# Cross-attention with layernorm: score matmuls on 32x128 tiles of the array, epsilon on GpSimd, and a new order within a pair

## The chip, the cores and the metric

The kernel runs on one core of a Trainium2 chip. A core has five engines with an instruction stream each: TensorE (PE; its weight loads are shown as PEld), VectorE (DVE), ScalarE (ACT), GpSimd (POOL) and SyncE (SP, which here only issues transfers). They work side by side and wait for one another through semaphores. The metric is the device time of one execution in microseconds (us). The kernel before takes 521.16 us (median of three: 519.04, 521.16, 522.03).

## The reference, cut to what matters

`x` is 8192 rows of 512 in float32 (four batches of 2048), `ctx` has 77 rows of 512 per batch and is key and value at once; the mask hides some of the 77 keys. There are 16 heads of 32.

```python
qs  = (x   @ wq).reshape(B, Lq, 16, 32).transpose(0, 2, 1, 3)
ks_ = (ctx @ wk).reshape(B, 77, 16, 32).transpose(0, 2, 1, 3)
vs  = (ctx @ wv).reshape(B, 77, 16, 32).transpose(0, 2, 1, 3)
scores = einsum('bhqd,bhkd->bhqk', qs, ks_) / sqrt(32)
scores = where(mask[:, None], -inf, scores)
attn   = einsum('bhqk,bhkd->bhqd', softmax(scores), vs)
out    = attn.transpose(0, 2, 1, 3).reshape(B, Lq, 512) @ wo + x
mu, var = mean(out), mean((out - mean(out)) ** 2)
y = (out - mu) / sqrt(var + 1e-5) * gamma + beta
```

## The kernel before, in words

The 8192 rows are 64 tiles of 128 rows, and the tiles go in pairs: pair n is tiles 2n and 2n + 1. Tiles 0 to 5 are done by a loop of their own at the start, together with the loads of the weights and the keys and values of the four batches. Pairs 3 to 26 (24 of them) all run through one list of words, the string `PAIR` (L47 to L51). Tiles 54 to 63 follow a longer written list, `ORDER`. Each word names a function, a tile, visit or pair relative to the current one, and at times a part. The order in which the words are issued is the order of each engine's instruction stream; there is no further scheduler, and buffers are given out in the same order.

What a pair does, with the letters of the words:

- `Q`, `q`: a *visit* computes q for 128 rows' worth of columns on TensorE (L186, 12 matmuls; float32 is made of high and low parts, hence three products of each) and VectorE copies it out of PSUM (L203). `g`, `i`, `j` load xT and split it into the two parts (load on SP, high part on ScalarE L175, low part on GpSimd L179).
- `S`, `D`: the scores of the pair, as q times keys, head by head (L310). The contraction is over the 32 columns of a head, so a matmul uses 32 rows of the array, and heads j = 0 to 3 of a group lie in four row groups of it. In the kernel before each score of 128 rows is two matmuls, for rows 0 to 63 and 64 to 127, each on a 32x64 tile of the array. Each float32 matmul shows as two records (two weight loads and two matmuls). A pair has 32 scores (16 heads, two tiles): `S` does 24 of them and `D` the other 8. They lie in six PSUM banks: four of their own, `sc` 0 to 3, and two shared ones, `sc_e` and `sc_f`.
- `T`: the maximum of a head's masked scores, on VectorE (L353; `T1.30` is for the two heads of the second tile that lie in `sc_f`); it writes masked scores to `pbuf` and the maxima `nm`. `e`: exponentials and their sums on ScalarE (L368). `r`: the sums' reciprocals on VectorE (L374). `n`: the multiplication by them on GpSimd (L379).
- `t`: a transpose on VectorE (L402) into `B`; `P`: its regrouping by 12 transfers on SP's queue (L414) into `PT`. `V`: attention times values, on TensorE (L448). `a`, `b`: its result is split into a high part AH on ScalarE (L497) and a low part AL on VectorE (L501).
- `O`: the output projection, 12 matmuls a tile on TensorE (L546). `+`: the residual, on VectorE (L549). `s`: mean and variance (L554, L559), and for the second tile of a pair the variance plus epsilon (L561, VectorE), its power −1/2 and two products (L562 to L564, GpSimd). `k`: scaling on ScalarE (L570). `f`: gamma and beta on GpSimd (L574, L575). `w` stores the tile (L578), `x` loads the residual (L518), both on SP.
- `L`, `B`: the mask of the next batch is loaded (L288, SP) and turned into a bias of −3e38 or 0 (L294, VectorE). This happens in three pairs, n = 6, 14 and 22 for `B`.

On TensorE a pair of the string is always S, D, O-6, O-5, Q5, Q6, V-2: the pair's own scores, the output of the tiles three pairs earlier, the visits of the next pairs, and av of the pair two earlier. PSUM has eight banks, handed out in a ring.

The lines that the change touches most:

```python
def score(t, g, j, half):
    r0 = (t % 4) * P + half
    return nc.tensor.matmul(
        scs[t][g, j][half : half + P // 2],
        qd[t // 4][q, g, r0 : r0 + P // 2], ...)
```

Of the kernel before, what the change touches and what calls it, by code (L numbers as in the profile page):

```python
# [13 lines left out]
ALU = mybir.AluOpType  # L14
# [3 lines left out]
P = 128  # L18
D = 512
# [7 lines left out]
GH = 4  # L27
# [7 lines left out]
EPS = 1.0e-5  # L35
# [5 lines left out]
JOIN = 6  # L41
# [3 lines left out]


PAIR = """  # L47
q4 k-8 a-3.1 f-8 i4 x-4 S T1.30 b-3.0 L T0.1 D e0.1 b-3.1 T0.0 T1.31 T1.3 x-3 T0.3 O-6 T1.10 T0.2 e0.0 T1.11 T1.14
+-6 T1.1 e0.3 s-6 O-5 t-1 e1.15 e0.2 r0 Q5 j4 g5 Q6 n0 e1.3 e1.10 +-5 q5 B e1.14 e1.1 e1.11 k-7 V-2 s-5 w-8 t0 r1 n1
P-1 f-7 w-7 a-2.0  # L50
"""  # L51
JOINT = """ a24.1 b24.0 b24.1 """

# [23 lines left out]
def xattn_layernorm(  # L77
# [15 lines left out]
    nc = tc.nc  # L93
# [35 lines left out]
    small = const.tile([P, 128], F32, name="small")  # L129
# [1 line left out]
    warm = ident.bitcast(BF16)  # L131
    ident = ident[:, :P]
    unit = ident.bitcast(F32R)
    mhalf, mneg, gates, meps = small[:, 0:2], small[:, 2:4], small[:, 4:5], small[:, 5:6]
    last_st = small[:, 8:20].rearrange("p (n s) -> p n s", n=2)
    pbuf = [const.tile([P, NP, PW], F32, name=f"pbuf{i}") for i in range(NPB)]

# [25 lines left out]
    fx, gx, qd, qp, bat, pts = {}, {}, {}, {}, {}, {}  # L163
    scs, nmax, sums, bts, at, pas = {}, {}, {}, {}, {}, {}
# [132 lines left out]
    def scores(t):  # L297
        nmax[t] = sb.tile([P, H], F32, tag="nm", bufs=3, name=f"nm_{t}")
        sums[t] = sb.tile([P, H], F32, tag="sum", bufs=3, name=f"sum_{t}")
        sc = [bank(f"sc_{t}_{j}") for j in range(GH)]  # L300
        scs[t] = {(g, j): sc[j][:, g * NK : (g + 1) * NK] for g in range(NG) for j in range(GH)}
        for g in range(NG):
            for half in range(0, P, P // 2):
                for j in range(GH):
                    score(t, g, j, half)

    def score(t, g, j, half):
        q = slice(HD * j, HD * (j + 1))
        r0 = (t % 4) * P + half
        return nc.tensor.matmul(  # L310
            scs[t][g, j][half : half + P // 2],
            qd[t // 4][q, g, r0 : r0 + P // 2],
            kct[q, g, t // TPB, keys_of(j)],
            start=True,
            stop=True,
        )

    def scores_pair(b):
# [6 lines left out]
        units = []  # L325
# [225 lines left out]
    def moments(t):  # L551
        b, tt = divmod(t, 2)
# [5 lines left out]
        mv, rn = mvs[b], rns[b]  # L558
        nc.vector.bn_aggr(mv[:, tt, :], st)  # L559
        if tt == 1:  # L560
            nc.vector.tensor_scalar(rn[:, 0, :], mv[:, :, 1], EPS, None, ALU.add)  # L561
            nc.gpsimd.tensor_tensor(rn[:, 0, :], rn[:, 0, :], mhalf, ALU.pow)  # L562
            nc.gpsimd.tensor_tensor(rn[:, 1, :], mv[:, :, 0], rn[:, 0, :], ALU.mult)
            nc.gpsimd.tensor_tensor(rn[:, 1, :], rn[:, 1, :], mneg, ALU.mult)  # L564
# [50 lines left out]
    def rsqrt_one(t):  # L615
        mv = mvs[t, 1]
        if t in summed:
            nc.gpsimd.tensor_scalar(mv[:, 2:3], mv[:, 1:2], 1.0 / D, meps, ALU.mult, ALU.add)
        else:
            nc.gpsimd.tensor_tensor(mv[:, 2:3], mv[:, 1:2], meps, ALU.add)  # L620
        nc.gpsimd.tensor_tensor(mv[:, 2:3], mv[:, 2:3], mhalf[:, :1], ALU.pow)

    def bias_one(t):
# [361 lines left out]
```

## Time and profile before

| | |
|---|---|
| median of three | 521.16 us |
| profiled execution | 520.62 us, span 518.8 us |
| granted TensorE clock, mean | 0.995 |
| TensorE busy | 498.5 us (96%), 6864 matmul records |
| VectorE / ScalarE / GpSimd busy | 469.7 / 471.3 / 420.1 us |
| score matmuls (L310) into the four own banks | 3312 records, mean 238 ns |
| instruction queue q8 | 54 packets, 0.88 MB |
| epsilon on VectorE (L561) | 24 times, mean 309 ns |

The span is the profiled execution from its first to its last event; 1.8 us lie outside it. Busy times overlap, since the engines work side by side: an engine at 96% of the span leaves little for others to shorten, unless what it waits for is found. A row of the table of waits reads: who waited, on which line, for which engine and line, with total, number and longest. "issue" is a wait that ended with no event that the profile shows. The chain of waits follows the work that ended last back through what released it, and its pieces are shown in order of time as start, length and what it was.

### The profile page before, as it was taken

To read this page: it belongs to the slowest core of one execution; us is meant where nothing else is said; L and a number is where in the kernel's file an instruction comes from. 1 tells how busy PE (TensorE), PEld (TensorE's weight loads), DVE (VectorE), ACT (ScalarE), POOL (GpSimd) and SP (SyncE) were. 2 spreads that over 40 slices of the span, in tenths; PEclk is the share of its full clock that TensorE was granted. 3 is DMA by queue.
4 is the path that set the end of the run, shared out by engine and by line. 5 is a ranking of instruction groups with operands and counts; after the bars stand their busy time and mean duration, and the time that the engine had idled before them with its cause. 6 is when DMAs were issued, how large, how long until landed. Compare 5 with 4: busy or idle time off the path is not lost.

```text
span 518.8 us, 20291 instructions
## 1 busy us (share of the span) xinstructions
PE 498.5 (96%) x6864; PEld 391.3 (75%) x6864; DVE 469.7 (91%) x2581; ACT 471.3 (91%) x2239; POOL 420.1 (81%) x359
## 2 busy tenths in 40 slices
PE   8999899999999999999999999989998999999994
PEld 6987578776777877776788777767876777777784
DVE  6698989899989999999999999998997899999997
ACT  6798989988999999998999999998999799999861
POOL 0659356887988989887998898887989688999894
PEclk9999999999999999999999999999998999999999
DMA  8946856696887888698688868788687778767665
GB/s 303 399 146 162 217 150 183 180 249 165 224 231 199 220 205 234 181 251 229 180 230 223 225 169 241 209 236 223 192 219 190 185 214 241 178 175 209 164 204 202
DMA packets 58279, 109.48 MB, mean 211 GB/s; under 512 B 9203, under 2 KB 10739, under 8 KB 58176
## 3 DMA queue, kind: packets, MB, share of 16 engines
q1 hardware_dynamic: 55776, 103.35, 71.4%
q0 software_dynamic: 1872, 4.20, 2.8%
q8 instruction: 54, 0.88, 0.8%
q10 hardware_dynamic: 528, 0.66, 0.4%
q14 instruction: 49, 0.40, 0.2%
HBM read 41.68 MB, written 16.78 MB: 113 GB/s over the span
## 4 chain that ended last, share of the span: by engine, by line
PE 79%; DVE 8%; DMA 5%; ACT 3%; issue 2%; SPq 2%; DVEq 0%; ACTq 0%
PE pq L186 27%; PE po L546 26%; PE pa L448 8%; PE sc L310 6%; PE sc L546 3%; DVE B L402 3%; DMA PT<-B 2%; ACT pbuf L368 2%; DVE pbuf L353 2%; SPq L414 2%; PE pv L252 2%; PE sc_e L310 2%; PE pk L212 1%; DMA out<-o 1%; PE pq L695 1%
## 5 line engine op out<-in xcount | busy, mean ns | idle before, releaser
L368 ACT ACTIVATE pbuf<-pbuf,nm 128x77 f32<-128x77 f32 x1024 | 352.0, 351 | 4.7 <-DVE nm L353 4.4
L368 ACT ACTIVATION_READ_ACCUMULATOR pbuf<-pbuf,nm 128x1 f32 x1024 | 196.7, 192 | 0.0
L379 POOL TENSOR_TENSOR pbuf<-pbuf,ri 128x1232 f32<-128x1232 f32 x63 | 142.1, 2256 | 53.6 <-DVE ri L374 53.0
L353 DVE CUSTOM_DVE_ANT_0 pbuf<-sc,mb 128x77 f32<-128x77 f32 x828 | 143.5, 233 | 6.4 <-PE sc L310 6.0
L186 PE MATMUL pq<-xth,wqh 128*128 128x512 f32 (+1 forms) x256 | 98.7, 386 | 0.0
L186 PE MATMUL pq<-xtl,wqh 128*128 128x512 f32 (+1 forms) x256 | 97.9, 382 | 0.0
L186 PE MATMUL pq<-xth,wql 128*128 128x512 f32 (+1 forms) x256 | 97.9, 382 | 0.0
L402 DVE STREAM_TRANSPOSE B<-pbuf 128x1280 f32<-128x1280 f32 x63 | 94.1, 1495 | 2.5 <-DMA PT<-B 1.2
L546 PE MATMUL po<-woh,AH 128*128 128x512 f32 x224 | 91.1, 407 | 0.0
L546 PE MATMUL po<-wol,AH 128*128 128x512 f32 x224 | 88.1, 393 | 0.6 <-issue 0.6
L546 PE MATMUL po<-woh,AL 128*128 128x512 f32 x224 | 87.1, 393 | 0.0
L353 DVE DVE_READ_ACCUMULATOR2_ANT nm<- 128x1 f32 x1024 | 84.5, 82 | 0.0
L575 POOL TENSOR_TENSOR o<-o,bet 128x512 f32<-128x512 f32 x53 | 68.5, 1293 | 4.2
L574 POOL TENSOR_TENSOR o<-o,gam 128x512 f32<-128x512 f32 x53 | 68.8, 1299 | 1.0 <-ACT o L570 1.0
L179 POOL TENSOR_TENSOR xtl<-xtf,xth 128x1024 fp32r<-128x1024 f32 x28 | 67.4, 2409 | 0.0
L310 PE MATMUL sc<-kct,q 32*64 32x77 f32 x3312 | 56.6, 238 | 5.2 <-issue 2.8
L448 PE MATMUL pa<-PT,vsb 96*32 96x256 f32 x960 | 58.2, 382 | 0.7 <-DMA PT<-B 0.3
L310 PEld LDWEIGHTS sc<-kct,q 32*64 32x64 f32 x3312 | 49.5, 130 | 11.3 <-issue 6.8
L186 PEld LDWEIGHTS pq<-xth,wqh 128*128 128x128 f32 x256 | 48.1, 188 | 9.7
L186 PEld LDWEIGHTS pq<-xth,wql 128*128 128x128 f32 x256 | 48.1, 188 | 9.4
L186 PEld LDWEIGHTS pq<-xtl,wqh 128*128 128x128 f32 x256 | 48.1, 188 | 9.2
L546 PEld LDWEIGHTS po<-woh,AH 128*128 128x128 f32 x224 | 42.4, 189 | 10.8 <-DVE ri L374 0.4
(170 smaller groups left out, 832.0 us busy)
## 6 DMA issues: line engine op xcount, KB each, us to landing
PT<-B SPq DMA_DIRECT2D x355, 128.0 KB
xtf<-xT SPq DMA_DIRECT2D x28, 512.0 KB
o<-x SPq DMA_DIRECT2D x56, 256.0 KB
out<-o SPq DMA_DIRECT2D x56, 256.0 KB
PT<-B POOLq DMA_DIRECT2D x16, 128.0 KB, 4.1
o_end<-x SPq DMA_DIRECT2D x7, 256.0 KB
out<-o_end SPq DMA_DIRECT2D x7, 256.0 KB
xtf<-xT SPq DMA_DIRECT2D x4, 256.0 KB
```

The source lines that it names most:

```text
L179: nc.gpsimd.tensor_tensor(l, fx.pop((g, c)), h.bitcast(F32), ALU.subtract)
L186: nc.tensor.matmul(pq, w[:, c, m * P : (m + 1) * P], r[:, c, rs], start=(n == 0), stop=(n == 11))
L252: nc.tensor.matmul(pv, ctx_s[c][i][:, r, :], v[c], start=(n == 0), stop=(n == 11))
L310: return nc.tensor.matmul(scs[t][g, j][half : half + P // 2], qd[t // 4][q, g, r0 : r0 + P // 2], kct[q, g, t // TPB, keys_of(j)], start=True,
L353: nc.vector.tensor_tensor_reduce(pb[:, i // 2, (i % 2) * NK : (i % 2 + 1) * NK], scs[t][g, j], mb[:, t % TPB, keys_of(h)], -1.0, CEIL, ALU ...
L368: nc.scalar.activation(p, p, AF.Exp, bias=nmax[t][:, i : i + 1], scale=-1.0, accum_out=sums[t][:, i : i + 1])
L379: nc.gpsimd.tensor_tensor(pv, pv, rv.to_broadcast((P, NP, 2, NK)), ALU.mult)
L402: nc.vector.transpose(bt.rearrange("p c q r -> p q c r"), pbuf[t % NPB].rearrange("p q (c r) -> p q c r", c=5),)
L448: nc.tensor.matmul(pas[b, g // 2][HD * j : HD * (j + 1), (g % 2) * BLK : (g % 2 + 1) * BLK], vsb[:, 2 * b // TPB, HD * h : HD * (h + 1)], ...
L546: nc.tensor.matmul(pos[t][:, cols], a[:, c, rs], w[:, c, cols], start=go, stop=done)
L574: nc.gpsimd.tensor_tensor(o, o, gam, ALU.mult)
L575: nc.gpsimd.tensor_tensor(o, o, bet, ALU.add)
```

## The change

Five things are edited.

1. A score of a pair is one matmul of 128 rows on a 32x128 tile of the array instead of two of 64 rows on 32x64 tiles: 32 matmuls a pair instead of 64. The single tiles at the start and the end keep the halves. In D the scores go in the order j = 0, 2, 3, 1.
2. Epsilon is added by GpSimd, from a column of constants two wide, instead of VectorE.
3. In the first pair (n = 3) O-6 stands before D.
4. In the words, `B` moves from late in the pair to right behind S, and `L` from the front to behind V-2.
5. The remaining words of VectorE, ScalarE, GpSimd and SP are reordered: f-8 behind j4, t-1 and t0 close together at the end, r0 and +-5 earlier, another order of the exponentials. On TensorE the order of a pair is as before.

```diff
--- before.py
+++ after.py
@@ -45,9 +45,9 @@
 
 
 PAIR = """
-q4 k-8 a-3.1 f-8 i4 x-4 S T1.30 b-3.0 L T0.1 D e0.1 b-3.1 T0.0 T1.31 T1.3 x-3 T0.3 O-6 T1.10 T0.2 e0.0 T1.11 T1.14
-+-6 T1.1 e0.3 s-6 O-5 t-1 e1.15 e0.2 r0 Q5 j4 g5 Q6 n0 e1.3 e1.10 +-5 q5 B e1.14 e1.1 e1.11 k-7 V-2 s-5 w-8 t0 r1 n1
-P-1 f-7 w-7 a-2.0
+q4 k-8 a-3.1 S B T1.30 b-3.0 T0.1 i4 e0.1 D x-4 T1.10 j4 T1.31 b-3.1 O-6 T0.2 T0.0 e0.2 T0.3 +-6 T1.3 T1.11 e0.0 x-3
+g5 e0.3 T1.14 e1.14 O-5 T1.1 e1.10 Q5 +-5 r0 s-6 e1.15 f-8 n0 s-5 Q6 w-8 q5 e1.1 t-1 V-2 L e1.11 t0 P-1 e1.3 k-7 r1
+n1 f-7 w-7 a-2.0
 """
 JOINT = """ a24.1 b24.0 b24.1 """
 
@@ -131,7 +131,7 @@
     warm = ident.bitcast(BF16)
     ident = ident[:, :P]
     unit = ident.bitcast(F32R)
-    mhalf, mneg, gates, meps = small[:, 0:2], small[:, 2:4], small[:, 4:5], small[:, 5:6]
+    mhalf, mneg, gates, meps = small[:, 0:2], small[:, 2:4], small[:, 4:5], small[:, 5:7]
     last_st = small[:, 8:20].rearrange("p (n s) -> p n s", n=2)
     pbuf = [const.tile([P, NP, PW], F32, name=f"pbuf{i}") for i in range(NPB)]
 
@@ -302,14 +302,14 @@
         for g in range(NG):
             for half in range(0, P, P // 2):
                 for j in range(GH):
-                    score(t, g, j, half)
-
-    def score(t, g, j, half):
+                    score(t, g, j, half, P // 2)
+
+    def score(t, g, j, r0, n):
         q = slice(HD * j, HD * (j + 1))
-        r0 = (t % 4) * P + half
-        return nc.tensor.matmul(
-            scs[t][g, j][half : half + P // 2],
-            qd[t // 4][q, g, r0 : r0 + P // 2],
+        at = (t % 4) * P + r0
+        nc.tensor.matmul(
+            scs[t][g, j][r0 : r0 + n],
+            qd[t // 4][q, g, at : at + n],
             kct[q, g, t // TPB, keys_of(j)],
             start=True,
             stop=True,
@@ -330,18 +330,15 @@
                 scs[t][g, j] = bk[:, at * NK : (at + 1) * NK]
             units.append(mine[6:] + mine[:6] if j % 2 == 0 else mine)
         for i in range(6):
-            for half in range(0, P, P // 2):
-                for j in range(GH):
-                    score(*units[j][i], j, half)
+            for j in range(GH):
+                score(*units[j][i], j, 0, P)
         held[b] = units
 
     def scores_rest(b):
         units = held.pop(b)
         for i in (6, 7):
-            for js in ((0, 2), (3, 1)):
-                for half in range(0, P, P // 2):
-                    for j in js:
-                        score(*units[j][i], j, half)
+            for j in (0, 2, 3, 1):
+                score(*units[j][i], j, 0, P)
 
     def maxima(t, lo, hi):
         pb = pbuf[t % NPB]
@@ -558,7 +555,7 @@
         mv, rn = mvs[b], rns[b]
         nc.vector.bn_aggr(mv[:, tt, :], st)
         if tt == 1:
-            nc.vector.tensor_scalar(rn[:, 0, :], mv[:, :, 1], EPS, None, ALU.add)
+            nc.gpsimd.tensor_tensor(rn[:, 0, :], mv[:, :, 1], meps, ALU.add)
             nc.gpsimd.tensor_tensor(rn[:, 0, :], rn[:, 0, :], mhalf, ALU.pow)
             nc.gpsimd.tensor_tensor(rn[:, 1, :], mv[:, :, 0], rn[:, 0, :], ALU.mult)
             nc.gpsimd.tensor_tensor(rn[:, 1, :], rn[:, 1, :], mneg, ALU.mult)
...
@@ -906,7 +903,11 @@
 
     def pair(n):
         u = 2 * n
-        for word in PAIR.split():
+        words = PAIR.split()
+        if n == JOIN // 2:
+            words.remove("O-6")
+            words.insert(words.index("D"), "O-6")
+        for word in words:
             op, k, part, queue = read(word)
             if op == "S":
                 scores_pair(n)
```

The first place is TensorE's stream in the first pair, n = 3, around D. In the names `sc_3_0` to `sc_3_3` are the pair's own four banks, `sc_3_e` and `sc_3_f` the shared ones, `po_0` and `po_1` the outputs of tiles 0 and 1. Before, the end of D and the output's start:

```order
L310 MATMUL sc_3_0_1056<-kct_71,q_1_529 64x77
L310 MATMUL sc_3_2_1058<-kct_71,q_1_529 64x77
L310 MATMUL sc_3_0_1056<-kct_71,q_1_529 64x77
L310 MATMUL sc_3_2_1058<-kct_71,q_1_529 64x77
L310 MATMUL sc_3_f_1061<-kct_71,q_1_529 64x77
L310 MATMUL sc_3_e_1060<-kct_71,q_1_529 64x77
L310 MATMUL sc_3_f_1061<-kct_71,q_1_529 64x77
L310 MATMUL sc_3_e_1060<-kct_71,q_1_529 64x77
L546 MATMUL po_0_1150<-woh_69,AH_0_953 128x512
L546 MATMUL po_0_1150<-wol_70,AH_0_953 128x512
```

Now, the end of the first output, D and the second output:

```order
L543 MATMUL po_0_1093<-woh_69,AH_0_953 128x512
L543 MATMUL po_0_1093<-wol_70,AH_0_953 128x512
L543 MATMUL po_0_1093<-woh_69,AL_0_954 128x512
L310 MATMUL sc_3_0_1053<-kct_71,q_1_529 128x77
L310 MATMUL sc_3_2_1055<-kct_71,q_1_529 128x77
L310 MATMUL sc_3_f_1058<-kct_71,q_1_529 128x77
L310 MATMUL sc_3_e_1057<-kct_71,q_1_529 128x77
L310 MATMUL sc_3_0_1053<-kct_71,q_1_529 128x77
L310 MATMUL sc_3_2_1055<-kct_71,q_1_529 128x77
L310 MATMUL sc_3_f_1058<-kct_71,q_1_529 128x77
L310 MATMUL sc_3_e_1057<-kct_71,q_1_529 128x77
L543 MATMUL po_1_1159<-woh_69,AH_0_953 128x512
```

D is eight matmuls of 128 rows, and the twelve of the first output stand ahead of it; in all other pairs D is followed by both outputs, as before.

The second place is VectorE's stream around the bias of batch 2, which pair 14 makes (`mb_2`). Before:

```order
L549 TENSOR_TENSOR o_23_3841<-po_23_4159,o_23_3841 128x512
L203 COPY q_8_3926<-pq_8_1_4181 128x512
L294 TENSOR_SCALAR mb_2_3806<-m8_2_3804 128x1536
L554 BN_STATS st_23_4247<-o_23_3841 128x6
L559 BN_AGGR mv_11_4156<-st_23_4247 128x2
L561 TENSOR_SCALAR rn_11_4157<-mv_11_4156 128x2
L402 STREAM_TRANSPOSE B_14_4255<-pbuf1_78 128x8x5x32
L374 RECIPROCAL ri_29_4257<-sum_29_4021 128x16
L203 COPY q_8_3926<-pq_8_2_4197 128x512
L353 ISA pbuf1_78,nm_31_4289<-sc_15_f_4296,mb_1_1646 128x77
```

Now:

```order
L399 STREAM_TRANSPOSE B_12_3387<-pbuf1_78 128x8x5x32
L399 STREAM_TRANSPOSE B_13_3627<-pbuf2_79 128x8x5x32
L371 RECIPROCAL ri_27_3647<-sum_27_3422 128x16
L203 COPY q_8_3583<-pq_8_0_3584 128x512
L294 TENSOR_SCALAR mb_2_3624<-m8_2_3622 128x1536
L350 ISA pbuf2_79,nm_29_3661<-sc_14_f_3668,mb_1_1720 128x77
L350 ISA nm_29_3661 128x1
L498 TENSOR_TENSOR AL_11_3654<-pa_11_0_3604,AH_11_3653 128x512
```

The bias stood behind the second visit's copy, with the statistics, a transpose, the reciprocal and the next pair's q copy behind it; now it stands between the pair's q copy and its first maxima, and the two transposes have come together ahead of the reciprocal.

The third place is SP's queue around the load of that mask. Before:

```order
L518 DMA o_22_3742<-x 128x512
L288 DMA m8_2_3804<-mask 128x1536
L518 DMA o_23_3841<-x 128x512
L170 DMA xtf_9_0_3924<-xT 128x1024
L578 DMA out<-o_18_3203 128x512
L414 DMA PT_12_3989<-B_12_3712 32x2x512 x12
```

Now:

```order
L515 DMA o_22_3472<-x 128x512
L515 DMA o_23_3519<-x 128x512
L170 DMA xtf_9_0_3521<-xT 128x1024
L575 DMA out<-o_18_2997 128x512
L288 DMA m8_2_3622<-mask 128x1536
L411 DMA PT_12_3629<-B_12_3387 32x2x512 x12
```

The mask's load was second in its pair's transfers; now it stands behind the store of tile 18, which waits for GpSimd's gamma and beta of that tile.

More of the change, by code (lines that the diff above doesn't have):

```diff
@@ L617, in rsqrt_one @@
         if t in summed:
-            nc.gpsimd.tensor_scalar(mv[:, 2:3], mv[:, 1:2], 1.0 / D, meps, ALU.mult, ALU.add)
+            nc.gpsimd.tensor_scalar(mv[:, 2:3], mv[:, 1:2], 1.0 / D, meps[:, :1], ALU.mult, ALU.add)
         else:
-            nc.gpsimd.tensor_tensor(mv[:, 2:3], mv[:, 1:2], meps, ALU.add)
+            nc.gpsimd.tensor_tensor(mv[:, 2:3], mv[:, 1:2], meps[:, :1], ALU.add)
         nc.gpsimd.tensor_tensor(mv[:, 2:3], mv[:, 2:3], mhalf[:, :1], ALU.pow)
```

## The prediction

> **What bounds the kernel now.** I read the page's busy shares first, then the chain of waits by engine, then the table of waits, then single stretches. The rows are the page's part 1, the chain's shares by engine, and four steps of the chain itself (start, duration, what):
>
> ```profile
> PE 498.5 (96%) x6864; PEld 391.3 (75%) x6864; DVE 469.7 (91%) x2581; ACT 471.3 (91%) x2239; POOL 420.1 (81%) x359
> PE 79%; DVE 8%; DMA 5%; ACT 3%; issue 2%; SPq 2%; DVEq 0%; ACTq 0%
> ...
> 245.87 5.67 PE po L546 x24
> 251.54 5.44 PE pq L186 x24
> 256.98 1.86 PE pa L448 x32
> 260.47 5.66 PE po L546 x24
> 333.98 5.68 PE po L546 x24
> ```
>
> TensorE is the bound. From 245.87 to 333.98 six pairs pass, 14.685 us each. In every one o_proj takes 5.67, the q visits 5.44 and av 1.86; what is left, 14.685 − 12.97 = 1.71, is the pair's scores. But a steady pair has little air on the other engines either. In the view by stretches (length, then busy of PE, PEld, DVE, ACT, POOL, then granted clock), one steady pair and one later stretch:
>
> ```profile
> 260.40:275.10 14.70, 14.70 (x212) 11.54 (x208) 13.86 (x80) 14.51 (x70) 13.11 (x12) 1.00 0.84 228
> 395.00:410.00 15.00, 13.64 (x62) 10.68 (x66) 11.47 (x68) 11.66 (x65) 10.37 (x9) 0.89 0.73 196
> ```
>
> ScalarE is busy 14.51 of 14.70: however short the scores get, a steady pair gives back only about 0.2 us before ScalarE sets the pace. So the gain has to come from places where PE stands still, and there are three kinds. The change acts on 24 pairs.
>
> **1. The score tiles: +2.9.** Single instructions of the timeline (start, duration, out<-in, array tile, shape):
>
> ```profile
> 245.80 0.50 PE L546 MATMUL po<-woh,AH 128*128 128x512 f32 x1
> 246.37 0.39 PE L546 MATMUL po<-woh,AL 128*128 128x512 f32 x1
> 258.78 0.28 PE L310 MATMUL sc_e<-kct,q 32*64 32x77 f32 x1
> 258.89 0.23 PE L310 MATMUL sc_e<-kct,q 32*64 32x77 f32 x1
> 258.96 0.23 PE L310 MATMUL sc_e<-kct,q 32*64 32x77 f32 x1
> 503.85 0.27 PE L529 MATMUL pa<-ident,xtl 128*128 128x128 f32 x1
> 503.96 0.27 PE L529 MATMUL pa<-ident,xth 128*128 128x128 f32 x1
> ```
>
> The first matmul after another shape shows its weight load: 0.50 − 0.39 = 0.11 us for 128 columns, 0.28 − 0.23 = 0.05 for 64. L529, whose matmuls are short, starts one every 0.11: it is bound by loads of 128 columns. Now eight score records start per 0.07 us (258.89 to 258.96), two 64-column halves of each of four row groups side by side, so that rhythm is the stream of 77 columns. A pair has 128 records (64 matmuls of two each), 16 such groups, 16 × 0.07 = 1.1; the rest of the 1.71 is the turn-over to and from other shapes and the tail D. Afterwards there are 64 records, 16 per row group, each behind a load of 128 columns: 16 × 0.11 = 1.76, with some 0.07 of last stream 1.83. That is 0.12 more per pair, × 24 = +2.9. Bounds: if 32-row loads hide behind the stream, 1.1 + 0.1, but ScalarE stops the gain at 0.2: −0.2 × 24 = −4.8. If a load has to wait for the matmul of its own row group, 16 × (0.11 + 0.07) = 2.9, 1.2 more per pair: +29. I take the value that L529's rows give.
>
> On this the Trainium skill, "TensorE: Matmul & The Clock Gate", says under "LDWEIGHTS (loading the stationary operand)" that a load's time follows its columns and not its rows, as assumed here. Its "The mechanism" (Part 3) says that a load overlaps running matmuls only when the row group differs, which would give the +29 bound; this trace disagrees, since L529 loads the full array every 0.11 us while its 0.27 us matmuls run. No run here shows it for 32x128.
>
> **2. Waits of PE for nothing that the profile shows: −6.7.** From the chain, with the q8 line of the page and of the 2 us before 349:
>
> ```profile
> 93.84 1.15 issue
> 141.15 0.65 issue
> 348.57 1.70 issue
> 394.68 1.69 issue
> 396.70 7.28 PE po L546 x24
> ...
> q8 instruction: 54, 0.88, 0.8%
> q8 instruction: 1, 0.02, 4.3%
> ```
>
> The four sum to 5.2, each inside or right after a score block. Queue 8 carries instructions: 0.88 MB are 13,728 × 64 bytes, PE's 6864 matmuls and 6864 loads, in 54 packets of some 256; and one packet lies beside the wait of 348.57. A score block now eats 256 instructions, a whole packet, in 1.7 us, where o_proj and q eat 96 in 11.1 us. I read the waits as PE having run through what was fetched. Afterwards a block has 128 instructions in 1.8 us: half a packet at half the rate, and the fetch that is late by up to 1.7 us has as much more time. I take all 5.2. After the wait at 394.68 o_proj ran 7.28 instead of 5.66 at a granted clock of 0.89 in that stretch: 1.6 more if the clock fell because of the stop. Together −6.7; bounds 0 (the waits have another source, or one packet stays late) and −6.7. I take the end: all four lie at score blocks, none elsewhere.
>
> The skill speaks against this: "Runtime: NRT & Kernel Launch", "Instruction fetch mechanics", says that fetch is hidden, as the sequencer issues more slowly than the buffer fills. By that the term is 0, a rival below.
>
> **3. The first pair (n = 3): −1.4.** Chain, waits and instructions there:
>
> ```profile
> 57.32 5.60 ACT pbuf L368 x32
> 62.95 0.25 DVE L374 RECIPROCAL ri<-sum 128x16 f32<-128x16 f32 x1 [0.73 <-ACT pbuf L368]
> 63.12 0.63 DVE L203 COPY q<-pq 128x512 f32<-128x512 f32 x1
> PE sc_f L310 <- DVE nm L353: 2.6, 1, 2.6
> 75.04 0.20 ACT L368 ACTIVATION_READ_ACCUMULATOR pbuf<-pbuf,nm 128x1 f32 x1
> 77.45 0.21 PE sc_e L310
> ```
>
> D writes the banks whose contents T1.30 reads first; T1.30 stands on VectorE behind a reciprocal that waits for exponentials until 62.95. PE stands 2.6 us. With O-6 ahead of D (12 matmuls, half of 5.67 = 2.8) that hole is filled, and PE would reach the next pair 2.6 earlier, at 74.8. But the next q evacuation stands behind a reciprocal that needs the exponentials ending at 75.24: + 0.2 + 0.63 gives 76.1 for S, against 77.45. So −1.4, the rest is ScalarE's; bounds 0 and −2.6.
>
> **4. The mask bias, in three pairs: 0.**
>
> ```profile
> L294 DVE TENSOR_SCALAR mb<-m x5: 552/950/2092, 16.0 to 359.7; 128x1536 bf16<-128x1536 uint8 x3, 128x768 bf16<-128x768 uint8 x2
> PE sc L310 <- DVE q L203: 2.4, 2, 1.2
> DVE pbuf L353 <- PE sc_f L310: 13.8, 17, 1.0
> ```
>
> B takes 2.0 us of VectorE (the longest of L294). Late in the pair it delayed the next q evacuation, and PE stood 1.2 twice: 2.4. Now it stands beside S, ahead of T1.30, and D waits for T1.30. VectorE has 0.8 of waiting for sc_f there (13.8 / 17), but its work in such a pair is 13.86 + 2.0, less the 0.3 of part 5, 15.6 against PE's 14.8: some 0.8 shows wherever B stands, × 3 = 2.4. Net 0. Bounds: −2.4 (VectorE catches up in the pairs around) and +1.2 (2.0 − 0.8 on D each time, 3.6 in all). Beyond it: L is now issued late, rival (c).
>
> **5. ε and the rest: 0.**
>
> ```profile
> L561 DVE TENSOR_SCALAR rn<-mv 128x2 f32<-128x2 f32 x24 | 7.4, 309 | 0.8
> L562 POOL TENSOR_TENSOR rn<-rn,small 128x2 f32<-128x2 f32 x24 | 16.8, 701 | 11.0 <-DVE rn L561 9.2
> L564 POOL TENSOR_TENSOR rn<-rn,small 128x2 f32<-128x2 f32 x24 | 4.7, 195 | 1.9
> ...
> PT<-B POOLq DMA_DIRECT2D x16, 128.0 KB, 4.1
> ```
>
> VectorE loses 0.31 a pair, which falls into its waits for sc_f; GpSimd gains between 0.2 (L564, a multiply) and 0.7 (L562, the power), and has 14.70 − 13.11 = 1.6 free in the steady pair. Without that cover it would be up to 24 × 0.7 = 17; and no gain is possible from VectorE while PE sets the pace. f-8, t-1, t0, r0 and the exponentials move within a pair. t-1 comes later and P-1's 12 transfers with it, at the pair's end: the same transfers take 4.1 us to land on GpSimd's queue, and av needs them 1.71 + 5.67 + 5.44 = 12.8 after the next S. I price these moves at 0.
>
> **Sum.** 2.9 − 6.7 − 1.4 + 0 + 0 = −5.2 on the profiled execution's 520.62 (span 518.8 and 1.8 around it): 515.4. The median shown is 521.16, 0.1% above; I say 515.7.
>
> **Rivals.**
> (a) *The loads hide.* For it: now 64-column loads leave no trace in the rhythm of 0.07. Against: L529's 0.11. Scores shrink, ScalarE takes over with its 0.2 a pair: −4.8 instead of +2.9, 515.7 − 7.7 = 508.
> (b) *The waits stay.* For it: the fetch may be late because the DMA engines are busy (0.84 in the steady stretch), which the change leaves. Against: all four lie at score blocks. The sum is 515.7 + 6.7 = 522.4, no change.
> (c) *Slower through the mask.* L is now behind V-2 and, in SP's queue, behind the store w-8, which waits for GpSimd's f-8. The page's rows:
>
> ```profile
> L379 POOL TENSOR_TENSOR pbuf<-pbuf,ri 128x1232 f32<-128x1232 f32 x63 | 142.1, 2256 | 53.6 <-DVE ri L374 53.0
> L575 POOL TENSOR_TENSOR o<-o,bet 128x512 f32<-128x512 f32 x53 | 68.5, 1293 | 4.2
> L179 POOL TENSOR_TENSOR xtl<-xtf,xth 128x1024 fp32r<-128x1024 f32 x28 | 67.4, 2409 | 0.0
> ```
>
> GpSimd does n1 from about S − 0.5 (2.3), f-7 (2 × 1.3), j4 (2.4), f-8 (2.6): 9.4 after S. With a landing like PT's 4.1 the mask is there at 13.5, and the next pair's B wants it at 14.7: 1.2 to spare. If GpSimd or the landing is late by more, B waits, with T1.30, all maxima, D and PE behind it. Two us beyond that, and a clock lowered by the stop (1.6, as after 394.68), are 3 × 3.6 = 10.8 in three pairs: 515.7 + 10.8 = 526.5; from 1.1 us too late on it is slower than before by 0.5%. For it: GpSimd's waits for ri (53.0 in all) show that it often starts late. Against: the order of before shows no wait of B for its mask, though with more time to spare.
> (d) *Slower through the loads*: the +29 bound, 515.7 − 2.9 + 29 = 542, decided as soon as a load of 128 columns waits for the matmul of its row group.
>
> **How the numbers follow.** Chances: forecast 0.53, (a) 0.15, (b) 0.15, (c) 0.11, (d) 0.06. What a measurement of this kernel can tell from no change is 0.5%, 2.6 us: faster is below 518.55, slower above 523.77. The forecast's own range is 511.5 to 519.5; it gives 0.44 faster and 0.09 same. (a) is faster; (b) gives 0.10 same, 0.01 faster and 0.04 slower; (c) 0.03 same, 0.08 slower; (d) 0.06 slower. Faster 0.60, same 0.22, slower 0.18. The range runs from (a)'s 507 to 523.5, past (b); it leaves out most of (c) and (d).
>
> **What would show it.** (1) po to pa: the gap between av's end and o_proj's start is 1.8 in steady pairs, and score starts per row group lie 0.11 apart; 0.07 means (a), 0.18 means (d). (2) q8 falls to about 42 packets and no wait named issue of 0.6 or more stays at scores. (3) No wait of 2.6 at sc_f near 61; S of the second pair near 76. (4) In three pairs PE waits some 0.8 ahead of D, none for q of 1.2. (5) GpSimd's wait for rn grows and costs nobody. A POOL or ScalarE row that ends PE's waits in every pair would make all of it wrong.

## The result and the profile after

The changed kernel took 517.0 us in the median (516.17 to 517.77, eight runs) against 519.33 (518.57 to 522.58, eight runs) of the kernel before on the same chip; the ratio of the means is 0.9941 (95% interval 0.9915 to 0.9966), about 3 us. The profiled execution took 517.48, its span 515.7 instead of 518.8. The page's busy shares, instruction queue and chain by engine:

```profile
PE 504.7 (98%) x5328; PEld 398.1 (77%) x5328; DVE 463.9 (90%) x2557; ACT 474.7 (92%) x2239; POOL 425.2 (82%) x383
q8 instruction: 42, 0.69, 0.6%
POOL 37%; PE 35%; DVE 10%; issue 7%; DMA 6%; SPq 4%; ACT 1%; POOLq 0%; DVEq 0%
```

The chain now runs through GpSimd for 37%, which reads as a new bound. It is not one. Each pair of it has 1.3 us of "issue" on GpSimd, a wait that the chain could not follow further, and the view by stretches (length, then busy of PE, PEld, DVE, ACT, POOL, then clock) shows TensorE busy all the time in a steady stretch:

```profile
260.00:275.00 15.00, 15.00 (x146) 11.82 (x145) 13.57 (x79) 14.66 (x71) 13.23 (x12) 1.00 0.80 213
```

Steps of the chain in the last third of the pairs (start, length, what):

```profile
341.17 5.14 DMA m<-mask
349.75 7.29 PE po L543 x24
366.30 5.67 PE po L543 x24
371.97 5.44 PE pq L186 x24
381.23 5.67 PE po L543 x24
396.15 5.67 PE po L543 x24
```

The period is 14.92 (396.15 − 381.23) instead of 14.685: every pair's scores have become 0.24 longer. The 7.29 is again an o_proj (the output projection, L543 here) at a lowered clock, at another place than before: from 349.68 to 356.88 the granted clock was 0.76, as it was from 396.60 to 403.80 in the kernel before. The waits of TensorE for "issue" above 0.6 are gone from the table of waits; of the kernel before it had, over the whole run and not only over the pairs:

```profile
PE sc_e L310 <- issue: 2.8, 2, 1.7
PE sc L310 <- issue: 2.8, 2, 1.7
PE po L546 <- issue: 0.6, 1, 0.6
```

The second row is 1.1 more than in the pairs alone: a fifth stop, at 464.20 in the tail (the tiles of `ORDER`), which the prediction did not count. The new stops of the changed kernel, and what VectorE's mask bias says of itself:

```profile
PE sc_f L310 <- DVE nm L350: 2.2, 3, 0.7
DVE mb L294 <- DMA m<-mask: 2.0, 2, 1.4
```

Where the 3.1 us of span went, by the starts of single matmuls in the two timelines (before, then after): up to the first pair's scores 59.89 and 59.38, −0.5; from there to the scores of tile 54, 365.93 and 364.60, −1.3; from there to the end 92.98 and 91.72, −1.3, which is the stop at 464.20. The −0.5 is no more than the scatter: variants of the changed kernel with the same work up to there start their first pair between 59.28 (e4 below) and 61.83 (e7). The −1.3 of the pairs is a difference of large terms:

- from the first pair's scores to the second pair's o_proj: −1.2, the longer scores of these two pairs included;
- scores of the other 22 pairs: 22 × 0.24 = +5.3;
- four stops: −6.1, from matmul start to matmul start less the usual distance, which is 0.9 more than the waits;
- mask pairs: +0.6 (three blocks of scores 1.17 longer than usual, 3.5, instead of two 1.45 longer, 2.9);
- one lowered clock in either trace: 0.

### The profile page after: what moved, and what is told of

It is laid out like the page before. It is cut to its first block, busy times and chain, and to the rows that moved or that the text cites. A ratio compares the mean times of both kernels' runs of the same rounds, so it can differ in the third digit from the quotient of the medians.

```text
span 515.7 us, 17190 instructions
## 1 busy us (share of the span) xinstructions
PE 504.7 (98%) x5328; PEld 398.1 (77%) x5328; DVE 463.9 (90%) x2557; ACT 474.7 (92%) x2239; POOL 425.2 (82%) x383
## 4 chain that ended last, share of the span: by engine, by line
POOL 37%; PE 35%; DVE 10%; issue 7%; DMA 6%; SPq 4%; ACT 1%; POOLq 0%; DVEq 0%
POOL pbuf L376 13%; PE pq L186 12%; PE po L543 8%; POOL o L572 7%; POOL o L571 7%; POOL xtl L179 7%; DVE pbuf L350 4%; DMA m<-mask 3%; PE sc L543 3%; PE pa L445 3%; PE sc L310 3%; SPq L411 3%; DVE B L399 2%; POOL rn L559 2%; PE pv L252 2%
## 5 line engine op out<-in xcount | busy, mean ns | idle before, releaser
L365 ACT ACTIVATION_READ_ACCUMULATOR pbuf<-pbuf,nm 128x1 f32 x1024 | 192.3, 188 | 0.0
L350 DVE CUSTOM_DVE_ANT_0 pbuf<-sc,mb 128x77 f32<-128x77 f32 x828 | 140.1, 233 | 6.9 <-PE sc L310 5.8
L399 DVE STREAM_TRANSPOSE B<-pbuf 128x1280 f32<-128x1280 f32 x63 | 91.8, 1488 | 0.4
L543 PE MATMUL po<-woh,AH 128*128 128x512 f32 x224 | 91.2, 407 | 0.0
L543 PE MATMUL po<-wol,AH 128*128 128x512 f32 x224 | 88.1, 393 | 0.0
L543 PE MATMUL po<-woh,AL 128*128 128x512 f32 x224 | 86.9, 392 | 0.0
L571 POOL TENSOR_TENSOR o<-o,gam 128x512 f32<-128x512 f32 x53 | 71.2, 1344 | 1.2 <-ACT o L567 1.2
L310 PE MATMUL sc<-kct,q 32*128 32x77 f32 (+1 forms) x2160 | 65.0, 257 | 0.3 <-DVE q L203 0.3
L310 PEld LDWEIGHTS sc<-kct,q 32*128 32x128 f32 (+1 forms) x2160 | 58.2, 160 | 6.3 <-issue 4.8
L543 PEld LDWEIGHTS po<-woh,AH 128*128 128x128 f32 x224 | 42.4, 189 | 10.7 <-DVE nm L350 0.4
```

The lines of the kernel that those rows point to most:

```text
L310: nc.tensor.matmul(scs[t][g, j][r0 : r0 + n], qd[t // 4][q, g, at : at + n], kct[q, g, t // TPB, keys_of(j)], start=True, stop=True,)
L350: nc.vector.tensor_tensor_reduce(pb[:, i // 2, (i % 2) * NK : (i % 2 + 1) * NK], scs[t][g, j], mb[:, t % TPB, keys_of(h)], -1.0, CEIL, ALU ...
L365: nc.scalar.activation(p, p, AF.Exp, bias=nmax[t][:, i : i + 1], scale=-1.0, accum_out=sums[t][:, i : i + 1])
L399: nc.vector.transpose(bt.rearrange("p c q r -> p q c r"), pbuf[t % NPB].rearrange("p q (c r) -> p q c r", c=5),)
L543: nc.tensor.matmul(pos[t][:, cols], a[:, c, rs], w[:, c, cols], start=go, stop=done)
L571: nc.gpsimd.tensor_tensor(o, o, gam, ALU.mult)
```

## The experiments

Theory F: TensorE stops at the end of a block of 256 of its own instructions when it has run through that block faster than the next one arrives. Rival to it: the stops come from the order of transfers. For the scores: 32x128 tiles are bound by loads, or by the stream. For the mask pairs: the mask lands late (rival (c) of the prediction), or VectorE's B cannot run beside GpSimd.

For each stop in the trace of the kernel before, here is how many matmuls, loads and semaphore instructions of TensorE had started until then, and how long the 256 up to there took.

| stop at | waits | instructions before it | modulo 256 | the block before it ran |
|---|---|---|---|---|
| 93.62 | 1.38 | 2497 | 193 | 1.94 us |
| 140.65 | 1.15 | 3777 | 193 | 1.62 us |
| 348.34 | 1.93 | 9665 | 193 | 2.20 us |
| 394.45 | 1.91 | 10945 | 193 | 1.78 us |
| 464.20 | 1.30 | 12993 | 193 | 3.39 us |

(The column "waits" is from matmul start to matmul start.) All stand at the same place modulo 256. In the pairs, the four blocks that ran in 2.2 us or less end in a stop; the next shortest, of 2.43, 2.78 and 2.97, end without. The fifth stop, in the tail, does not fit this: its block ran 3.39.

### Only the tile shape undone, and only the tile shape done

```diff
@@ changed kernel, scores_pair: e1
-            for j in range(GH):
-                score(*units[j][i], j, 0, P)
+            for half in range(0, P, P // 2):
+                for j in range(GH):
+                    score(*units[j][i], j, half, P // 2)
@@ changed kernel, scores_rest: e1
-            for j in (0, 2, 3, 1):
-                score(*units[j][i], j, 0, P)
+            for js in ((0, 2), (3, 1)):
+                for half in range(0, P, P // 2):
+                    for j in js:
+                        score(*units[j][i], j, half, P // 2)
@@ kernel before, scores_pair; scores_rest likewise: e2
-            for half in range(0, P, P // 2):
-                for j in range(GH):
-                    score(*units[j][i], j, half)
+            for j in range(GH):
+                score(*units[j][i], j, 0, P)
...
```

> The changed kernel with only the tile shape undone (pairs' scores in halves of 64 rows, D in the old order). Theory (PE stops at the end of a block of 256 of its own instructions when that block ran in less than about 2.2 us): from av's end to o_proj's start 1.7 us instead of 1.95, a steady pair 14.7 instead of 14.93, so 24 x 0.24 = 5 to 6 us less there; q8 back at 54 packets; three to six stops of 0.6 to 1.9 us come back, each at the end of a 256-instruction block that held nearly a whole score block, not necessarily in the pairs of before. Sum: 517.0 - 5.5 + (3 to 8) = 515 to 519. Rival (the four stops of before came from its order of transfers, not from the instructions): no stop, 511.5. Rival (the tile shape costs nothing): stops back and pairs still 14.93, 522.

> The kernel before with only the pairs' scores on 32x128 tiles; order, epsilon and first pair as before. Theory: 42 q8 packets, no stop named issue of 0.6 us or more in a pair or in the tail (-5.2 and -1.3), every pair's scores 0.24 longer (+5.8): 519.3 - 0.7 = 518 to 519, so no measurable change, and the rest of the gain lies in the new order. Rival (the stops come from transfers): they stay, 519.3 + 5.8 = 525. Rival (the tile shape is the whole gain): 516 to 517.

Undone in the changed kernel (e1): ratio 0.9999 (0.9964 to 1.0034) to before, against 0.9941 with it (another set of runs, whose interval it touches) and 0.9925 for e4 below, which has the tile shape and was measured in the same set; so the tile shape was worth about 0.6 to 0.7% there. Done alone in the kernel before (e2): 1.0024 (0.9991 to 1.0057), no measurable gain. Both traces show stops where theory F puts them. In e1 q8 is back at 54 packets and five stops of 0.9 to 2.1 are back (91.84, 138.70, 186.85, 394.72, 438.86), all at 192 or 193 modulo 256; steady pairs take 14.60 to 14.7. Four of the five stand in the pairs, after blocks of 1.78 to 2.30 us; the last and longest, at 438.86, stands in the tail after a block of 3.71, so the 2.2 us of the expectation is not the whole condition. In e2 no such stop is left and the pairs take 14.93. Waits of TensorE in e1, and an o_proj to o_proj distance in it:

```profile
PE pq L186 <- issue: 1.7, 1, 1.7
PE sc_e L310 <- issue: 1.5, 1, 1.5
PE sc L310 <- issue: 1.4, 1, 1.4
PE sc_f L310 <- issue: 1.2, 1, 1.2
PE po L546 <- issue: 0.5, 1, 0.5
...
261.78 5.67 PE po L546 x24
276.38 5.67 PE po L546 x24
```

So the tile shape trades about 6 us of longer scores for 6 to 8 us of stops; it pays only by the little that is left over and, as the section on the clock below argues, by what can follow a stop. The rival of the transfers is out: in e2 all transfers are those of before.

### The same stops, moved

```diff
@@ kernel before, scores() of the single tiles: e3
+        n = P if t in (4, 5) else P // 2
         for g in range(NG):
-            for half in range(0, P, P // 2):
+            for r0 in range(0, P, n):
                 for j in range(GH):
-                    score(t, g, j, half)
+                    score(t, g, j, r0, n)
...
```

> The kernel before, but tiles 4 and 5, which come before all pairs, have their scores on 32x128 tiles: 128 PE instructions fewer ahead of the pairs, so every block of 256 ends 128 instructions later in the program. Theory: moving the block ends by 128 on the times of before leaves one block of about 2.1 us in the pairs (it ends near 197 us, in the pair whose scores start near 198) where there were four below 2.2; so the stops near 93, 140, 348 and 394 are gone, at most one or two others stand elsewhere: 519.3 - 3 to 5 = 514.5 to 516.5. Rival (transfers or the order): the four stops stay where they are, 519.3 within 1.

Ratio 0.9906 (0.9873 to 0.994). The four stops of the pairs are gone, and one stands where it was forecast, at 199.22, index 5313, again 193 modulo 256, after a block of 2.12 us; a second, of 0.6, came after a block of 2.62 at 293.62, and none in the tail.

```profile
201.23 0.28 PE L311 MATMUL sc<-kct,q 32*64 32x77 f32 x1 [1.79 <-issue]
```

Sixty-four matmul records and as many loads fewer ahead of all pairs, in tiles that the pairs never see again, gained about as much as the whole change. Only the position of the block ends had moved (the first pair's scores start at 59.77 instead of 59.89).

The packets of queue 8 show the rest of theory F. The trace holds the start and end of each, one for a block, and they are matched here in order. Before the stop at 348.34, for example, the packet runs from 347.51 to 348.88, and TensorE goes on at 350.27. Of the 534 block ends after 50 us in the twelve traces of this document, 17 end in a stop of 0.5 us or more. In all 17 TensorE goes on 1.25 to 1.6 us after the end of the packet, and the packet ended at most 0.92 before the block did. Where the packet had ended 1.6 us or more before the block's end, there is no stop (one block lies between, with 1.05 and a gap of 0.28). So what TensorE waits for is the next block of instructions; how long the block before ran decides only together with when its packet comes.

### What bounds a score matmul on 32x128

```diff
@@ changed kernel, score(): e9 (each score in two, 39 and 38 keys)
+        keys = keys_of(j)
+        cut = [0, NK] if n < P else [0, 39, NK]
+        for k0, k1 in zip(cut, cut[1:]):
...
-            scs[t][g, j][r0 : r0 + n],
+                scs[t][g, j][r0 : r0 + n, k0:k1],
...
-            kct[q, g, t // TPB, keys_of(j)],
+                kct[q, g, t // TPB, keys.start + k0 : keys.start + k1],
...
```

> The changed kernel with every pair score cut along the keys into two matmuls of 39 and 38 columns that load the same 128 columns of q: twice the loads and half the stream for each. Theory (32x128 score matmuls are bound by their weight loads, 0.11 us each per row group): a pair's scores take 3.5 us or more from first to last start instead of 1.75, some 24 x 1.75 = 42 us more, near 560. Rival (bound by the stream of 77 columns): first to last start stays near 1.8, 517 to 520 with some instruction stops.

592.13 us (one run), more than expected. Scores take 3.59 from first to last start instead of 1.75, twice as long with half the stream each, so the stream does not bound them. One row group's starts, in the changed kernel and then here,

```profile
257.17 0.27 PE L310 MATMUL sc_e<-kct,q 32*128 32x77 f32 x1
257.28 0.27 PE L310 MATMUL sc_e<-kct,q 32*128 32x77 f32 x1
257.39 0.27 PE L310 MATMUL sc_e<-kct,q 32*128 32x77 f32 x1
```

```profile
112.50 0.28 PE L313 MATMUL sc_e<-kct,q 32*128 32x39 f32 x1
112.61 0.28 PE L313 MATMUL sc_e<-kct,q 32*128 32x38 f32 x1
112.72 0.28 PE L313 MATMUL sc_e<-kct,q 32*128 32x38 f32 x1
```

are both 0.11 apart. A fixed price of 0.11 for each matmul would give the same; against it stands the kernel before, whose matmuls behind loads of 64 columns start every 0.07. So the loads of 128 columns bound them. The pairs are 16.79 where nothing else happens, 24 × 1.86 = 45 more; of the remaining 30 some 27 are o_proj blocks at a lowered clock (mean clock 0.935), below.

### The mask pairs

```diff
@@ changed kernel, PAIR: e4 (L early again)
-q4 k-8 a-3.1 S B T1.30 b-3.0 T0.1 ...
+q4 k-8 a-3.1 S B T1.30 b-3.0 L T0.1 ...
-... V-2 L e1.11 ...
+... V-2 e1.11 ...
```

> The changed kernel with the load of the mask (L) back at its early place, B left beside S. Theory A (the mask lands late: VectorE's B waits 1.4 and 0.7 us for it, and PE stands about 1 in these pairs): the waits vanish, PE's stops in two of three pairs shrink to 0.3 or less, 517.0 - 1.5 = 515.5. Theory B (B cannot finish while GpSimd runs its multiply of L376 beside it, and ends 0.85 us after that multiply whenever it started): B starts earlier and lasts longer, 2 to 2.6 us, and ends where it did; PE's stops of 1.0 stay in all three pairs, 517.0 within 0.5.

Ratio 0.9925 (0.9891 to 0.9958), the same as the changed kernel within the intervals. The start-to-start stops of TensorE are 0.99 in all three pairs, as in the changed kernel. VectorE and GpSimd in one of these pairs:

```profile
104.92 2.69 DVE L294 TENSOR_SCALAR mb<-m 128x1536 bf16<-128x1536 uint8 x1
107.53 0.23 DVE L350 CUSTOM_DVE_ANT_0 pbuf<-sc_f,mb 128x77 f32<-128x77 f32 x1
```

```profile
104.54 2.25 POOL L376 TENSOR_TENSOR pbuf<-pbuf,ri 128x1232 f32<-128x1232 f32 x1 [1.35 <-DVE ri L371]
106.75 1.99 POOL L571 TENSOR_TENSOR o<-o,gam 128x512 f32<-128x512 f32 x1
```

B starts beside GpSimd's multiply, and ends 0.82 us after that multiply does (104.92 + 2.69 = 107.61; 104.54 + 2.25 = 106.79). Alone it takes 0.95 (the shortest whole B of before). GpSimd's next instruction lasts 1.99 instead of 1.30, as long as B needs. It is the same wherever B meets an instruction of GpSimd: in ten of the twelve traces 28 whole B's do, they last 1.1 to 2.7 us, and each ends 0.81 or 0.82 after GpSimd's instruction. So B and GpSimd's instructions exclude each other for whole instructions. In the changed kernel "DVE mb <- DMA m<-mask" named the mask's landing, and the time at which T1.30 began was the same to 0.1 us without that wait: the last releaser by the profile was not what held it up.

The Trainium skill's page "SBUF — State Buffer" ("SBUF: two separate sides") says just this: VectorE, in modes that use two ports, and GpSimd share a pair of ports, the one that starts first holds it for a whole instruction, and the other is blocked. The trace agrees, here with the 0.82 us, and below; which mode B runs in, no trace shows.

### Hybrid scores, and the bias on GpSimd

```diff
@@ changed kernel, scores_pair: e5 (S on halves, D on 32x128)
-            for j in range(GH):
-                score(*units[j][i], j, 0, P)
+            for half in range(0, P, P // 2):
+                for j in range(GH):
+                    score(*units[j][i], j, half, P // 2)
@@ e5, further: e6 (bias in two halves of eight tiles, two pairs, ahead of r1; L early)
+    def mask_bias_pool(b, ts):
+        mb, m8 = bat[b]
+        nc.gpsimd.tensor_scalar(mb[:, ts], m8[:, ts], MASKED, None, ALU.mult)
...
-q4 k-8 a-3.1 S B T1.30 ...
+q4 k-8 L a-3.1 S T1.30 ...
-... V-2 L e1.11 t0 P-1 e1.3 k-7 r1
+... V-2 e1.11 t0 P-1 e1.3 k-7 B r1
...
```

> The changed kernel with S (24 of a pair's 32 scores) back on halves of 64 rows and only D (8 scores) on 32x128 tiles. A pair then has 224 PE instructions in its scores, less than a block of 256. Theory (a stop comes where a block of 256 instructions runs in less than about 2.2 us): from the trace of the kernel with all halves, with D's instructions halved, no block is shorter than 2.6 us wherever the block ends fall, so no stop of 1 us or more, at most one or two below it; scores from av's end to o_proj's start 1.6 to 1.7 instead of 1.95, a steady pair 14.6 to 14.7: 24 x 0.25 to 0.3 = 6 to 7 less than the changed kernel, ratio to before about 0.981 to 0.983. Rival (the score blocks are short of instructions whenever they hold 64-row halves): stops of 1 to 2 us stay in 4 or more pairs, ratio 0.99 or more. Rival (ScalarE sets the pace as soon as the scores shrink): steady pairs stay above 14.8, ratio 0.99.

> The kernel of the hybrid scores, with the mask bias made by GpSimd in two halves, each ahead of its multiply at the end of a pair, and L early; VectorE has no B any more. Theory (T1.30, and D and PE behind it, wait because VectorE's B ends only 0.85 us after GpSimd's multiply): the three stops of 1 to 1.3 us in the pairs with B vanish, 3 to 4 us less than the hybrid alone (ratio lower by 0.006 to 0.008). Rival (PE's stop there has another source, such as AH or the q copy): stops stay. Rival (GpSimd has no room): its half delays its multiply and the next transposes, and PE waits for PT: no gain or a loss of up to 3 us.

e5: 0.9986 (0.9943 to 1.0029); no stop for instructions in any pair, as forecast, but no gain. Steady pairs take 14.84, not 14.6 to 14.7: from S to o_proj is 1.86 instead of 1.95. The 24 scores of S take 1.20 from first to last start in halves (first pair of e1) and 1.36 on 32x128 (first pair of the changed kernel): the rhythm of 0.07 per eight records, which the prediction read off their first starts and which would make 0.84 of the 1.20, is not held. What slows it was not tried. And the mask pairs became worse:

```profile
PE sc_f L310 <- DVE nm L351: 5.0, 3, 2.1
```

Here the mask did land late, and B then met GpSimd's next instruction:

```profile
107.40 1.20 DVE L294 TENSOR_SCALAR mb<-m 128x1536 bf16<-128x1536 uint8 x1 [2.62 <-DMA m<-mask]
106.52 1.26 POOL L572 TENSOR_TENSOR o<-o,gam 128x512 f32<-128x512 f32 x1
```

B started at 107.40, when GpSimd's multiply had long ended (106.55), and ended 0.82 after gamma (108.60 and 107.78). Two of the three stops were 2.33 from start to start, and each was followed by an o_proj of 6.95 instead of 5.36. Rival (c), which did nothing in the changed kernel, was real one edit further on.

e6: 0.9879 (0.9824 to 0.9933), 1.07% less than e5 in the same set. All three stops are gone, and TensorE's table of waits has no wait for VectorE's maxima left (a stop for instructions of 0.8 stands in the tail, as one of 0.5 does in e5). That is 2.3 + 2.3 + 1.2 of stops less, and the two lowered clocks; it was expected to be 0.6 to 0.8%.

### The first pair, and epsilon

```diff
@@ changed kernel, pair(): e7
-        if n == JOIN // 2:
-            words.remove("O-6")
-            words.insert(words.index("D"), "O-6")
@@ changed kernel, moments(): e8
-            nc.gpsimd.tensor_tensor(rn[:, 0, :], mv[:, :, 1], meps, ALU.add)
+            nc.vector.tensor_scalar(rn[:, 0, :], mv[:, :, 1], EPS, None, ALU.add)
```

> The changed kernel with D back ahead of O-6 in the first pair. Theory: PE stands 2.6 us in front of the first pair's D again, and the second pair's o_proj starts 1.2 to 1.4 later relative to the first pair's scores (18.1 in the changed kernel, 19.3 before); one time some 1.3 above the changed kernel's, within the scatter of single runs. Rival (ScalarE's exponentials decide the second pair's start in any case): it starts at the same distance, 18.1.

> The changed kernel with epsilon added by VectorE again. Theory (epsilon hides on either engine while PE sets the pace): steady pairs 14.93 as in the changed kernel, PE's stops of 1.0 in the three pairs with B unchanged; one time within the scatter, 516 to 519. Rival (VectorE is short of time, or its 0.3 us delays the maxima or the q copy): steady pairs 15.0 or more, or the stops grow by 0.3.

e7 (one run, 521.45): TensorE stands 2.3 in front of D again, and from the first pair's scores (61.83) to the second pair's o_proj (83.03) it is 21.2. Of that 1.6 is a lowered clock (an o_proj of 7.28 right behind the stop), so 19.6 against 18.1: the move is worth 1.5, and in this run 3.1.

e8 fell far from what was expected: 544.76 us (one run). Steady pairs took 15.7 instead of 14.93. Epsilon's line, and one of them beside GpSimd:

```profile
L558 DVE TENSOR_SCALAR rn<-mv x24: 760/1853/1904, 73.6 to 444.6; 128x2 f32<-128x2 f32 x24
```

```profile
185.49 1.86 DVE L558 TENSOR_SCALAR rn<-mv 128x2 f32<-128x2 f32 x1
```

```profile
185.07 2.26 POOL L376 TENSOR_TENSOR pbuf<-pbuf,ri 128x1232 f32<-128x1232 f32 x1
```

An operation on two numbers a row takes 1.86 us, because it begins 0.4 into GpSimd's multiply and ends with it (187.35 and 187.33). Behind it stands the copy of q, and TensorE waits for that. In the kernel before, the same instruction had a median of 0.365 and at most 0.371 (its row by line): its order had it stand where GpSimd waited. So epsilon was free there, and would cost 0.8 a pair in the new order, where n0 runs on GpSimd at that time: 24 × 0.8 = 19 of the 28 us, and lowered clocks behind longer stops another 6.6 (four slow o_proj blocks instead of one). Giving epsilon to GpSimd is what makes the new order usable.

### All halves, with the block ends placed

```diff
@@ e6, scores_rest: e10 (WHOLE = pairs 5, 13 and 24)
-            for j in (0, 2, 3, 1):
-                score(*units[j][i], j, 0, P)
+            if b in WHOLE:
+                for j in (0, 2, 3, 1):
+                    score(*units[j][i], j, 0, P)
+                continue
+            for js in ((0, 2), (3, 1)):
+                for half in range(0, P, P // 2):
+                    for j in js:
+                        score(*units[j][i], j, half, P // 2)
```

> The kernel with hybrid scores and the mask bias on GpSimd, but D back on halves of 64 rows too in 21 of the 24 pairs; pairs 5, 13 and 24 keep D on 32x128 tiles, so that no block of 256 PE instructions ends just behind a whole score block. Theory (stops only where a block of 256 runs in under some 2.2 us): from the trace of that kernel, with 32 instructions more and 0.17 us less in each of the 21 pairs, the shortest block of the pairs is 2.8 us, so no stop of 1 us or more in any pair although a pair's scores again hold 256 instructions; steady pairs 14.67 instead of 14.84, 21 x 0.17 = 3.6 less: ratio to before about 0.981. Rival (any pair with 256 instructions in its scores can stop, wherever its blocks end): 3 to 5 stops of 1 to 2 us come back, no gain or a loss against 0.988. Rival (ScalarE holds the pace): steady pairs stay at 14.84, 0.988.

510.75 us (510.26 to 512.32, six runs), ratio 0.978 (0.9738 to 0.9822): faster than before by 1.8 to 2.6%, and below the changed kernel's interval. It has 54 packets of instructions again and steady pairs of 14.67:

```profile
271.38 5.66 PE po L555 x24
286.05 5.69 PE po L555 x24
...
PE sc L315 <- DVE q L204: 1.9, 3, 1.0
PE po L555 <- issue: 0.4, 1, 0.4
```

One stop for instructions is left, 0.8 from start to start, after a block that ran in 2.23 us where 2.8 had been worked out: three waits for the q copy, of up to 1.0, had moved the pairs. ScalarE is late more often in this kernel (VectorE's reciprocal waits for its exponentials nine times, up to 1.9, against three times in the changed kernel), so ScalarE is near.

## Why the prediction was right, and where not

The time (515.7 said, 517.0 measured) lay in the range and the gain had the right sign; it was about 3 us instead of 5.5. That the time came so close is partly luck. The 515.7 was worked out from a median of three runs, 521.16, where eight runs of the kernel before gave 519.33. And of the terms, the scores (2.9 too low), the lowered clock (1.6 that did not come) and the mask (0.6) were too hopeful by 5.1, while the tail's stop (1.3), the longer stops (0.9), the first pair (0.3) and the scatter ahead of it (0.5) brought 3.0 back that nobody had priced. Term by term:

1. **Scores, +2.9: mis-sized, +5.8.** The mechanism was right (a load of 128 columns every 0.11, e9), and the bounds of a hidden load and of a load that waits for its row group are both out: the rule of the Trainium skill quoted there would have made it 2.9 a pair, and it is 1.95. What failed is "with some 0.07 of last stream". The turn-over between shapes, which the working had itself counted for the old tiles ("the turn-over to and from other shapes"), was left out for the new. From the first start to the second it is 0.17 instead of 0.11, and 0.20 from the last start to o_proj; so 1.95 and not 1.83, against 1.70 before.
2. **Stops named issue: right in cause and size.** −5.2 was taken; it was all of it (−6.1 from start to start), and 1.3 more in the tail, which had been missed by reading the waits in the pairs alone. That half the rate of instructions would be enough was right too: no stop is left at a score block. The Trainium skill ("Runtime: NRT & Kernel Launch", "Instruction fetch mechanics") calls this cost mostly hidden; measured here are 0.5 to 2.1 us at 17 ends of blocks of 256 instructions. The −1.6 of the lowered clock was not gained between the two profiled runs: a lowered clock follows a long stop only by chance, and the changed kernel's profile has one too, behind a stop for the mask. On average some of it may be there, since the mean granted clock is 0.996 over the eight runs of the changed kernel and 0.991 to 0.992 over the runs of the kernel before in the three later sets; of the first set only one clock of the kernel before is known, 0.995. (5.2 and 1.6 are 6.8, not 6.7, which changes nothing.)
3. **First pair, −1.4: right**, −1.2 between the two traces, where the longer scores of two pairs (0.5) are in it, and 1.5 by e7.
4. **Mask pairs, 0: about right (+0.6), by a wrong working.** "[I]ts work in such a pair is 13.86 + 2.0", of VectorE: B's 2.0 is not work but 0.95 and a wait for GpSimd, so it could be had away altogether (e6). So that 0.8 in front of D came as forecast (0.7 as a wait, 1.0 from start to start) was luck. Rival (c) had the right place and a wrong cause: early or late, the mask changed nothing in this kernel (e4).
5. **Epsilon, 0: right for the sum, wrong as reasoning.** "VectorE loses 0.31 a pair, which falls into its waits" took the duration as fixed. It depends on what GpSimd does beside it: 0.17 to 1.9 us. The edit was no free choice but a condition of the new order, and left out it costs some 28 us (e8, one run).

The rivals (a), (b) and (d) are out by the traces, and (c) by e4. That the gain came out at about half is due to term 1 and to the clock of term 2; and the two terms of the tile shape, longer scores and fewer stops, cancel almost wholly, so that it gave nothing alone (e2).

## What to carry to other kernels

Count the bound engine's instructions between its stops: if they all stand at one remainder modulo 256, the stops are waits for the next block of instructions, and moving the block ends, by more or fewer instructions anywhere ahead (128 here), can be cheaper than fewer, slower instructions. A VectorE instruction whose duration varies from one pass of the loop to the next, and which ends with GpSimd's or always the same time after it, is waiting and not working; give the work to GpSimd or put it where GpSimd is idle. When a row of the waits names a transfer, take the transfer away before believing it.

## What the runs showed of the hardware that was not expected

**The clock falls, by chance, after a long stretch of scores and stop.** Over all twelve traces, take the time from the first score of a pair to its o_proj and look at that o_proj (5.35 from first to last start at the full clock). Under 3.05 us: 230 blocks, none slow. From 3.05 to 3.85: 10 of 42 slow. Above 3.85: 18 of 20. Slow means 6.5 to 8.1, mostly 6.95 (the granted clock was 0.76 over the two shown above), so a stop that brings a pair above 3 us costs its own length and, by chance, 1.6 more. It fits the scatter of the kernel before on one chip, 515.60 in a run with a mean clock of 0.999 and 523.15 in one with 0.986, and that of the last kernel, which hardly stops: 510.3 to 512.3, 0.996 to 0.998. That the length decides is read from these traces; no run changed the length alone.

**Stops come where the packet of instructions is late, and not only behind short blocks.** In the pairs of all traces ten blocks ran in 2.30 us or less, and all ten end in a stop of 0.8 to 2.0; of the longer ones, from 2.43 on, one does (2.62, with 0.6). But in the tail six blocks of 3.3 to 3.7 end in one too, in before, e1, e5, e6 and twice in e9. From the first instruction of a block to TensorE's next start behind the stop pass 2.8 to 5.8 us, in three parts: until the packet starts (0.3 to 2.95), its transfer (0.9 to 1.8), and 1.25 to 1.6 behind it. The first varies most: at the stops in the tail it is 2.16 in before and 2.95 in e1, in the pairs at most 1.38. What holds the packet back there stays open.
